# A hand-written beat table for the middle of a transformer block on one core: two alternating tables, and the split of keys or queries on GpSimd

## The chip, the core and the metric

The kernel runs on one core of one Trainium2 chip. The metric is device time in microseconds of one execution. Of the kernel before, three runs are known: 737.49, 738.01 and 738.19 us (median 738.01). A separate execution was profiled: 737.81 us, of which 736.0 us lie between its first and its last instruction.

Engines are named as the profile names them: PE (TensorE, the matmuls), PEld (its weight loads), DVE (VectorE), ACT (ScalarE), POOL (GpSimd), SP (SyncE, which here only issues DMAs).

## The reference: what is computed

One block of a diffusion transformer on x of 16 batches x 256 tokens x 256 features, in float32. The modulation vectors come from `cond`, 16 heads have 16 features each:

```python
x_norm = modulate(_ln(x), shift_a, scale_a)
q, k, v = jnp.split(x_norm @ W_qkv + b_qkv, 3, axis=-1)              # then 16 heads of 16
attn_w = softmax(einsum('bhqd,bhkd->bhqk', q, k) * scale)
x = x + gate_a[:, None] * (einsum('bhqk,bhkd->bhqd', attn_w, v) @ W_proj + b_proj)
q_c = _ln(x) @ W_qc + b_qc                                            # cross attention, 256 context rows
k_c, v_c = jnp.split(_ln(context) @ W_kvc + b_kvc, 2, axis=-1)
x = x + (softmax(q_c k_c * scale) v_c) @ W_cproj + b_cproj
h = gelu(modulate(_ln(x), shift_m, scale_m) @ W_mlp1 + b_mlp1) @ W_mlp2 + b_mlp2
x = x + gate_m[:, None] * h
```

## The kernel before

**Units.** An attention of one batch is a unit: 16 self attentions (names with `s`, `k`, `q`) and 16 cross attentions (names with `c`, `kc`, `qc`). They are done in the order of `seq` (line 785): five self attentions first, then self and cross attention in turn. From unit 5 to unit 25 an odd unit is a self attention and an even unit a cross attention. The MLP of all batches follows behind the units.

**High and low parts.** Matmuls run on float32r. To keep float32 accuracy an operand is cut in two: a high part that is rounded, and a low part, the rest (`xTh`/`xTl`, `h_k`/`l_k`, `h_q`/`l_q`). For a transposed activation ACT copies the PSUM tile to SBUF (`y`), POOL casts it to the high part and subtracts to get the low part (`cut`, line 380). For keys and queries ACT writes the high part (`high`, line 503: two ACTIVATE, bias added) and DVE the low part (`low`, line 508: two SCALAR_TENSOR_TENSOR that read PSUM and the high part). SP then sends rows of both by DMA into `big`, a stack in which 16 features of a head stand as three parts in 63 or 64 partitions (`send`, line 521).

**A unit's own work.** `s_tile` (line 691) multiplies queries by keys into two PSUM banks, `s` bank 0 and bank 1, and DVE takes the row maximum of each bank (`mx`, TENSOR_REDUCE). The maxima are transposed (`psm`), ACT negates them (`m`), and a DMA puts them as a 64th row into `big`. `t_part` (line 734) multiplies again, transposed and with the maximum subtracted, into `st`; ACT takes the exponent of the two halves of `st` in one instruction (`exp`, line 745, `pt`). `av_part` (line 768) multiplies by the values (`o`), ACT copies out (`oT`), PE transposes (`psA`), DVE divides by the row sums (`norm`, line 629), PE transposes again (`psT_a..`), and the projection follows (`ps_P`).

**Two lanes on PE.** Nearly all matmuls between have 64 rows, so that two run at once, one in each half of the array. `beside` (line 475) merges two lists of pieces, x for the upper half and y for the lower one, by the length issued so far; a matmul counts 1, a half transpose 0.53. PE takes them in this one order: a matmul that waits holds up both lanes.

**The beats.** A unit n is eight beats, and `PLAN` (line 1106) says what each holds: words before the lanes, the words of lane x, those of lane y, and words behind. Each beat has one `s` tile pair (of unit n+1) and one `t` pair (of unit n). Q12 is twelve matmuls of a lane of a projection (Q, K, V, P), T, U, A0, A1 and a are groups of half transposes, m0 and m1 those of the maxima; o0 (behind beat 4) and o1 (behind beat 0) are blocks of 16 matmuls with all four quarters of the array at work. The other words issue work of ACT, DVE, POOL or SP at that place: E the exponent of the beat, kh/kl/kH/kL and qh/ql/qH/qL the high and low parts of keys and queries (of unit n+2) and their DMAs, Te/Tc, Ue/Uc and ae/ac copies and cuts, n0/n1 the norms, c1/c2, e5/e6, s1/s6/s7 the three steps of layer norms, add and gate residual work of POOL, Vk the copy of V. Every engine takes its instructions in the order of the program (`InOrder`, line 40): a word's place decides what stands ahead of it on its engine.

The words that a sentence can't say:

```python
("c1", "s t Q12", "t P2 s P10", "L1 ld kL E"),          # beat 1 of PLAN, for odd and even units alike
("", "s t T pe A1 V3", "s t Q4 T A1 Q1", "hadd E L2 Te Tc c2"),
```

Of the kernel before, what the change touches and what calls it, by code (L numbers as in the profile page):

```python
# [16 lines left out]
P = 128  # L17
# [4 lines left out]
def pixart_block(  # L22
# [460 lines left out]
    def to_stack(W, src, bias, dst, which, name):  # L483
# [50 lines left out]
        o.low_pool = low_pool  # L534
        o.high, o.low = high, low
        o.send_high = lambda: [send(f, part) for part in range(2) for f in range(KC)]
# [63 lines left out]
    def build_post(u):  # L600
# [51 lines left out]
        def end():  # L652
            t1 = work.tile([P, NT, H], F32, tag="t1", name=f"t1_{name}")
            o.t1 = t1
            ACT.copy(t1.rearrange("p t h -> p (t h)"), o.ps)

        def add():
            t1 = o.t1
            if u.kind == "s":
# [96 lines left out]
    def exps():  # L756

        for f in later:
            f()
        later.clear()  # L760
# [133 lines left out]
    def to_hidden(b, c, src, park):  # L894
# [11 lines left out]

        o.high = o.keep = keep
        o.low = o.send_high = o.send_low = lambda: None
        return o
# [97 lines left out]
    for n, v in (("0", u0), ("1", u1), ("2", u2)):  # L1007
        word["T" + n + "t"], word["T" + n + "h"], word["T" + n + "l"] = v.T[0].parts
        word["T" + n + "p"] = v.T[0].low_pool
        for c in "KQ":  # L1010
# [4 lines left out]
            for f in range(KC):  # L1015
                for q, k in enumerate("xyl"):
                    word[f"{c}{n}{k}{f}"] = lambda o=o, q=q, f=f: o.send(f, q)
                    word[f"{c}{n}{k}{f}p"] = lambda o=o, q=q, f=f: o.send(f, q, POOL)
            word[c + n + "s"] = lambda o=o: [o.send(f, q) for f in range(KC) for q in range(3)]
    for n in range(2):  # L1020
# [71 lines left out]
    def visit(n, k, home=sp):  # L1092
# [6 lines left out]
        if n >= 0:  # L1099
            bank = sp if n == nu - 1 and k % 2 else st  # L1100
            t = [t_part(units[n], k, par, bank) for par in range(2)]
            later.append(lambda: exp(units[n], k, bank))
        return s, t

    none = (), ()
    PLAN = [
# [8 lines left out]
    ]  # L1115
    lanes = {}

    def beat(n, k):
# [21 lines left out]
        def attention(v, hf):  # L1140
# [6 lines left out]
        do = {  # L1147
            "E": exps, "o1": lambda: attention(prev, 1), "o0": lambda: attention(cur, 0),
            "kh": on(q2, lambda: q2.K.high()), "kl": on(q2, lambda: q2.K.low()),
# [7 lines left out]
            "ae": on(p1, lambda: p1.aT.evac()), "ac": on(p1, lambda: p1.aT.cut()),  # L1157
            "n1": on(p1, lambda: p1.norm(1)), "n0": lambda: cur.post.norm(0),
            "pe": on(p2, lambda: p2.end()), "hadd": on(p2 and (p2.n == nu - 3), lambda: (p2.add(), p2.store())),
            "add": on(p3, lambda: p3.add()), "gate": on(p1, lambda: p1.gate()),  # L1160
# [3 lines left out]
            "c1": on(lc or ls and ls.kind == "m", lambda: lc.ln[0].steps[0]() if lc else mlp_bias(ls.b)),  # L1164
            "c2": on(lc, lambda: [f() for f in lc.ln[0].steps[1:]]),
            "s1": on(ls, lambda: ls.ln[0].steps[0]()),
            "s6": on(ls, lambda: ls.ln[0].steps[1]()),
            "s7": on(ls, lambda: ls.ln[0].steps[2]()),
            "e5": on(early, lambda: early.ln[1].steps[0]()),
            "e6": on(early, lambda: [f() for f in early.ln[1].steps[1:]]),  # L1170
            "L1": on(late, lambda: lx.ln[1].steps[0]()), "L2": on(late, lambda: lx.ln[1].steps[1]()),
# [31 lines left out]

        before, x, y, then = PLAN[k]
        for w in before.split():
# [137 lines left out]
```

## Time and profile before

| | |
|---|---|
| three runs | 737.49, 738.01, 738.19 us |
| profiled execution | 737.81 us; span 736.0 us |
| PE busy | 727.4 us (99%), granted clock 0.999 |
| DVE, ACT, POOL busy | 567.6 (77%), 562.6 (76%), 521.6 us (71%) |
| DVE row maxima `mx<-s` | 504 instructions, 684 ns each |
| ACT exponents `pt<-st` | 252 instructions, 1027 ns each |

The span begins with some 45 us of set-up, the units fill the stretch to about 545 us, and the MLP the rest. The two `o` blocks of a unit are easily found in the chain of waits, so that they serve as milestones: those of unit 16 start at 303.7 and 311.8 us, of unit 17 at 319.7 and 328.0, of unit 18 at 335.9. A pair of units takes 32.25 us.

PE's busy share counts an instruction from its start to a modelled end, with two lanes overlapping, so 99% does not say that both lanes are filled: what a lane loses shows in the distance between the starts of its matmuls.

### The profile page before, as it was taken

How to read it: one execution, taken by the hardware profiler on the slowest of the kernel's cores; microseconds unless marked ns; L12 is line 12 of the kernel's file. 1: busy time of each engine (PE TensorE's matmuls, PEld its weight loads, DVE VectorE, ACT ScalarE, POOL GpSimd, SP SyncE). 2: the span in 40 equal slices, each digit the busy share in tenths (PEclk: the TensorE clock that was granted, in tenths of full speed). 3: DMA queues.
4: the chain of work that ended last, by engine and by line, in shares of the span. 5: the costliest groups of instructions: out<-in, count | busy, mean ns of one | idle time of the engine just before them, and what ended most of it. 6: DMA issues, size and time to landing. Idle time of an engine off the chain costs nothing.

```text
span 736.0 us, 25389 instructions
## 1 busy us (share of the span) xinstructions
PE 727.4 (99%) x10092; PEld 641.9 (87%) x10092; DVE 567.6 (77%) x1164; ACT 562.6 (76%) x976; POOL 521.6 (71%) x639
## 2 busy tenths in 40 slices
PE   8999999999999999999999999999999999999997
PEld 8778888888888888888888888888889999999997
DVE  5888888989888888888888989888746765565542
ACT  4277898888888888888888888888887766666663
POOL 6757576858567575856757687778568898898872
PEclk9999999999999999999999999999999999999999
DMA  6855445543545454354545555454321644443420
GB/s 207 204 148 146 134 129 137 141 124 97 155 112 157 131 143 136 103 153 112 159 129 138 139 143 164 121 164 121 118 74 30 166 134 110 121 129 92 118 81 33
DMA packets 108906, 94.81 MB, mean 129 GB/s; under 512 B 36914, under 2 KB 92756, under 8 KB 108788
## 3 DMA queue, kind: packets, MB, share of 16 engines
q1 hardware_dynamic: 108308, 92.27, 45.3%
q8 instruction: 80, 1.31, 0.8%
q0 software_dynamic: 192, 0.52, 0.3%
q10 hardware_dynamic: 288, 0.39, 0.2%
q14 instruction: 38, 0.31, 0.1%
HBM read 30.38 MB, written 11.86 MB: 57 GB/s over the span
## 4 chain that ended last, share of the span: by engine, by line
PE 94%; DVE 2%; issue 1%; ACT 1%; DMA 1%; POOL 1%; SPq 0%; POOLq 0%; ACTq 0%; DVEq 0%
PE s L51 17%; PE st L51 16%; PE o L51 16%; PE ph L51 11%; PE ps_qc L51 4%; PE ps_q L51 4%; PE ps_kc L51 3%; PE ps_P_s L51 3%; PE ps_k L51 3%; PE ps_v_c L51 3%; PE ps_v_s L51 3%; PE ps_P_c L51 2%; PE ps_h L51 1%; PE psT_q L51 1%; PE psA_s L51 1%
## 5 line engine op out<-in xcount | busy, mean ns | idle before, releaser
L51 DVE TENSOR_REDUCE mx<-s 128x2 f32<-128x512 f32 x504 | 324.6, 684 | 63.7 <-PE s L51 57.1
L51 ACT ACTIVATE pt<-st 128x1024 f32<-128x1024 f32 x252 | 258.9, 1027 | 17.7 <-PE st L51 11.8
L51 PE MATMUL s<-big 63*128 63x256 f32 (+1 forms) x1024 | 184.4, 298 | 0.6 <-DVE mx L51 0.4
L51 PEld LDWEIGHTS s<-big 63*128 63x128 f32 (+1 forms) x1024 | 133.6, 186 | 19.9 <-DVE l_kc L51 6.6
L51 PE MATMUL st<-big 64*128 64x256 f32 (+1 forms) x1024 | 134.2, 298 | 0.3 <-ACT pt L51 0.2
L51 PE MATMUL o<-pt,v 128*32 128x256 f32 x2048 | 123.8, 382 | 0.1
L51 PEld LDWEIGHTS st<-big 64*128 64x128 f32 (+1 forms) x1024 | 96.0, 185 | 16.2 <-issue 12.9
L51 POOL TENSOR_TENSOR hl<-hf,hh 128x512 fp32r<-128x512 f32 x64 | 85.1, 1335 | 29.1 <-ACT hh L51 29.0
L51 PEld LDWEIGHTS o<-pt,v 128*32 128x32 f32 x2048 | 60.2, 109 | 41.4 <-PE psm L51 0.2
L51 ACT ACTIVATE hh<-ph,bT 128x256 fp32r<-128x256 f32 x114 | 47.8, 473 | 23.3 <-PE st L51 10.0
L51 ACT ACTIVATE hf<-ph,bT 128x256 f32<-128x256 f32 x114 | 47.6, 469 | 21.2 <-PE ph L51 21.2
L51 ACT COPY oT<-o 128x512 f32<-128x512 f32 x63 | 36.9, 586 | 33.9 <-PE o L51 33.9
L51 PE MATMUL s<-big,hh 128*128 128x256 f32 x256 | 46.8, 282 | 0.0
L51 PE MATMUL st<-big,hh 128*128 128x256 f32 x256 | 46.5, 281 | 0.0
L51 PE MATMUL ph<-wqch,wself 128*128 128x256 f32 x224 | 44.4, 282 | 0.0
L51 PE MATMUL ph<-wkch,wself 128*128 128x256 f32 x224 | 44.3, 281 | 0.0
L51 PE MATMUL ps_k<-xTh_s,wself 64*128 64x256 f32 (+1 forms) x232 | 43.9, 294 | 0.0
L51 DVE TENSOR_SCALAR xn_m<-x,mv_m,rs_m 128x256 f32<-128x256 f32 x28 | 28.8, 1067 | 19.0 <-POOL rs_m L51 19.0
L51 POOL CAST xTh_ac<-y_ac 128x512 fp32r<-128x512 f32 x15 | 9.2, 612 | 46.6 <-ACT y_ac L51 46.6
L51 POOL CAST xTh_c<-y_c 128x512 fp32r<-128x512 f32 x16 | 9.8, 612 | 45.5 <-ACT y_c L51 45.5
L51 PE MATMUL ps_q<-xTh_s,wself 64*128 64x256 f32 (+1 forms) x240 | 39.8, 283 | 0.4 <-DVE l_q L51 0.4
L51 PE MATMUL ps_v_s<-wself,xTh_s 64*128 64x256 f32 x224 | 39.2, 294 | 0.0
(249 smaller groups left out, 2528.5 us busy)
## 6 DMA issues: line engine op xcount, KB each, us to landing
big<-h_kc SPq DMA_DIRECT2D x64, 128.0 KB
big<-h_qc SPq DMA_DIRECT2D x64, 128.0 KB
big<-h_k SPq DMA_DIRECT2D x62, 128.0 KB
big<-h_q SPq DMA_DIRECT2D x62, 128.0 KB
big<-l_k SPq DMA_DIRECT2D x32, 128.0 KB
big<-l_q SPq DMA_DIRECT2D x32, 128.0 KB
g<-gd SPq DMA_DIRECT2D x16, 256.0 KB
c<-in_ctx_dram SPq DMA_DIRECT2D x16, 256.0 KB
```

The source lines that it names most:

```text
L51: i = f(*a, **k)
```

## The change

Units 6 to 21 (8 even, 8 odd) are done by two new tables, `PLANS[0]` for even n and `PLANS[1]` for odd n; the other units keep the old table, which is now `PLANS[2]`. All words of the old table stay in each of the new ones, but their places differ, many now stand inside a lane, and four steps are changed:

- **Keys of even units (`kr`, `kc`) and queries of odd units (`qr`, `qc`).** With `rows` ACT writes the rows with bias as float32 to SBUF (two ACTIVATE as before), with `cut` POOL casts them to the high part and subtracts for the low part. The two DVE instructions of `low` are gone there. Queries of even units and keys of odd units are made as before.
- **F** issues the exponent as two instructions, one for each half of `st`, in place of one (twice a unit).
- The layer norms' middle step is parted: statistics (DVE) apart from the power (POOL): c2/c3/c4, s6/s7/s8, e6/e7/e8.
- Lane lengths of some beats differ (Q, V and K matmuls moved over a beat's edge).

`gated_end`, the words pd, add2, store2 and the sends by ACT are defined and not used by the tables.

```diff
@@ to_stack
+        def rows():
+            o.hi = work.tile([P, KC, N], F32R, tag="qkh", name=f"h_{name}", bufs=3)
+            o.lo = work.tile([P, KC, N], F32R, tag="qkl", name=f"l_{name}", bufs=3)
+            for f in range(KC):
+                ACT.activation(o.lo[:, f].bitcast(F32), o.ps[:, f * N:(f + 1) * N], AF.Identity, bias=bias[f])
+
+        def cut():
+            POOL.tensor_copy(o.hi, o.lo.bitcast(F32))
+            POOL.tensor_tensor(o.lo, o.lo.bitcast(F32), o.hi, ALU.subtract)
@@ exp
-    def exp(u, pair, st):
+    def exp(u, pair, st, apart=False):
         u.pt[pair] = work.tile([P, 2, NT, N], F32, tag="pt", name=f"pt_{u.n}_{pair}", bufs=5)
-        if isinstance(st, list):
+        if apart or isinstance(st, list):
             for r in range(2):
-                ACT.activation(u.pt[pair][:, r].rearrange("p c n -> p (c n)"), st[r], AF.Exp, scale=SCALE)
+                ACT.activation(u.pt[pair][:, r].rearrange("p c n -> p (c n)"), side(st, r), AF.Exp, scale=SCALE)
             return
@@ the tables
-    PLAN = [
+    FROM, TO = 6, 22
+    PLANS = [[("", "s t kr m1 E", "m1 add t s", "m1s"),
+              ("kc o1", "s t Q12", "t s P12 E c1", "gate"),
...
+              ("", "t e5 ql s a m0 K6", "t s V4 a V2 m0 F", "ae"),
...
+              ("", "s Te V1 t V1 hadd Tc F V7", "Q2 t s Q5 qr", ""),
+              ("qc", "s t qH", "s t", "E c4 L3 o0"),
+              ("", "t store s a E K2 m0 K2", "n1 t s qL V4 a V1 m0", "ae ac s1 e5 m0s"),
+              ("", "s lc K1 t K3 A0 E K4 U", "V3 t begin V2 s U s6 V2 e8 A0", ""),
...
@@ beat
-        before, x, y, then = PLAN[k]
+        before, x, y, then = PLANS[n % 2 if FROM <= n < TO else 2][k]
```

What the tables move is seen in the order of the engines' instructions. First DVE in unit 16 (even), from behind beat 4 to beat 7; `l_qc` is the low part of queries, `st_q`/`mv_q` the statistics of a layer norm, `mx<-s_110` and `mx<-s_111` the maxima of the two banks. Before:

```order
L51 SCALAR_TENSOR_TENSOR l_qc_6649<-ps_qc_6488,bT,h_qc_6611 128x256 x2
L51 TENSOR_REDUCE mx_83<-s_110 128x2
L51 TENSOR_REDUCE mx_83<-s_111 128x2
L51 BN_STATS st_q_6703<-xg_4229 128x6 x2
L51 TENSOR_REDUCE mx_83<-s_110 128x2
L51 TENSOR_REDUCE mx_83<-s_111 128x2
L51 BN_AGGR mv_q_6740<-st_q_6703 128x2 x2
```

And in the changed kernel:

```order
L51 BN_STATS st_q_6674<-xg_4277 128x6 x2
L51 SCALAR_TENSOR_TENSOR l_qc_6677<-ps_qc_6499,bT,h_qc_6633 128x256 x2
L51 TENSOR_REDUCE mx_83<-s_110 128x2
L51 TENSOR_REDUCE mx_83<-s_111 128x2
L51 BN_AGGR mv_q_6725<-st_q_6674 128x2 x2
L51 TENSOR_REDUCE mx_83<-s_110 128x2
L51 TENSOR_REDUCE mx_83<-s_111 128x2
```

The statistics went ahead of the maxima of beat 5, to where PE is in its `o` block, and the aggregation ahead of those of beat 6.

Second, POOL in the first beats of unit 16; `t_s`, `xg` are the residual work of a self attention (words add and gate), `xTh_s`/`xTl_s` the parts that the K matmuls of unit 19 read in beat 5, `rs_c` a layer norm's power. Before:

```order
L51 TENSOR_TENSOR t_s_6157<-t_s_6157,g_5614 128x512
L51 TENSOR_TENSOR xg_5723<-xg_5723,t_s_6157 128x512
L51 TENSOR_TENSOR xg_6470<-x_4638,g_6361 128x512
L51 CAST xTh_s_6565<-y_s_6562 128x512
L51 TENSOR_TENSOR xTl_s_6566<-y_s_6562,xTh_s_6565 128x512
L51 TENSOR_SCALAR rs_c_6572<-mv_c_6569 128x2
L51 TENSOR_TENSOR rs_c_6572<-rs_c_6572,mhalf 128x2
```

And in the changed kernel:

```order
L51 TENSOR_TENSOR t_s_6156<-t_s_6156,g_5595 128x512
L51 TENSOR_TENSOR xg_5779<-xg_5779,t_s_6156 128x512
L51 CAST h_kc_6457<-l_kc_6458 128x512
L51 TENSOR_TENSOR l_kc_6458<-l_kc_6458,h_kc_6457 128x512
L51 TENSOR_TENSOR xg_6530<-x_4651,g_6346 128x512
L51 TENSOR_SCALAR rs_c_6582<-mv_c_6579 128x2
L51 TENSOR_TENSOR rs_c_6582<-rs_c_6582,mhalf 128x2
L51 CAST xTh_s_6599<-y_s_6576 128x512
L51 TENSOR_TENSOR xTl_s_6600<-y_s_6576,xTh_s_6599 128x512
```

The split of the keys `h_kc`/`l_kc` is new in this queue, and it and the power now stand ahead of the cast `xTh_s`.

Third, PE in unit 17 (odd), at the edge from beat 2 to beat 3; `psA` are half transposes of lane y, `ps_q` matmuls of lane y, `ps_v` of lane x. Before:

```order
L51 MATMUL psA_c_6906<-ident,oT_3_6837 128x64 x3
L51 MATMUL ps_q_6853<-xTh_s_6565,wself 128x256
L51 MATMUL s_110<-big_75 128x256
L51 MATMUL ps_q_6853<-xTh_s_6565,wself 128x256
L51 MATMUL s_110<-big_75 128x256
L51 MATMUL st<-big_77 128x256 x4
```

And in the changed kernel:

```order
L51 MATMUL psA_c_6927<-ident,oT_3_6859 128x64 x4
L51 MATMUL s_110<-big_75 128x256
L51 MATMUL ps_q_6872<-xTh_s_6599,wself 128x256
L51 MATMUL s_110<-big_75 128x256
L51 MATMUL ps_q_6872<-xTh_s_6599,wself 128x256
L51 MATMUL ps_v_s_6934<-wself,xTh_s_6599 128x256
L51 MATMUL st<-big_77 128x256 x4
```

A matmul of `ps_v` now stands ahead of `st`, and one of `ps_q` went from ahead of `psA` to behind `s`.

More of the change, by code (lines that the diff above doesn't have):

```diff
@@ L534, in to_stack @@
         o.low_pool = low_pool
-        o.high, o.low = high, low
+        o.high, o.low, o.rows, o.cut = high, low, rows, cut
         o.send_high = lambda: [send(f, part) for part in range(2) for f in range(KC)]
@@ L653, in end, with gated @@
             t1 = work.tile([P, NT, H], F32, tag="t1", name=f"t1_{name}")
-            o.t1 = t1
+            o.t1, o.gated = t1, False
             ACT.copy(t1.rearrange("p t h -> p (t h)"), o.ps)
+        def gated():
+            o.t1 = o.out = work.tile([P, NT, H], F32, tag="t1", name=f"t1_{name}")
+            o.gated = True
+            ps = o.ps.rearrange("p (t h) -> p t h", t=NT)
+            if u.kind == "s":
+                DVE.tensor_tensor(o.t1, ps, bc_t(G[b][:, 0]), ALU.mult)
+            else:
+                DVE.tensor_tensor(o.t1, ps, X1[b], ALU.add)
+        o.gated_end = gated
         def add():
             t1 = o.t1
+            if o.gated:
+                if u.kind == "s":
+                    X1[b] = o.xg
+                    POOL.tensor_tensor(X1[b], o.xg, t1, ALU.add)
+                return
             if u.kind == "s":
@@ L754, in pixart_block, with exps @@
     later = []
-    def exps():
+    def exps(apart=False):
         for f in later:
-            f()
+            f(apart)
         later.clear()
@@ L905, in keep @@
             M[b].kept.append(c)
-        o.high = o.keep = keep
-        o.low = o.send_high = o.send_low = lambda: None
+        o.high = o.keep = o.rows = keep
+        o.low = o.cut = o.send_high = o.send_low = lambda: None
         return o
@@ L1018, in pixart_block @@
                     word[f"{c}{n}{k}{f}p"] = lambda o=o, q=q, f=f: o.send(f, q, POOL)
+                    word[f"{c}{n}{k}{f}a"] = lambda o=o, q=q, f=f: o.send(f, q, ACT)
             word[c + n + "s"] = lambda o=o: [o.send(f, q) for f in range(KC) for q in range(3)]
@@ L1101, in visit @@
             t = [t_part(units[n], k, par, bank) for par in range(2)]
-            later.append(lambda: exp(units[n], k, bank))
+            later.append(lambda apart: exp(units[n], k, bank, apart))
         return s, t
     none = (), ()
-    PLAN = [
[8 rows of a table removed]
-    ]
+    FROM, TO = 6, 22
+    PLANS = [[("", "s t kr m1 E", "m1 add t s", "m1s"),
[23 rows of a table added]
     lanes = {}
@@ L1158, in beat @@
             "n1": on(p1, lambda: p1.norm(1)), "n0": lambda: cur.post.norm(0),
+            "pd": on(p2, lambda: p2.gated_end()), "kr": on(q2, lambda: q2.K.rows()), "kc": on(q2, lambda: q2.K.cut()),
+            "qr": on(q2 and hasattr(q2, "Q"), lambda: q2.Q.rows()), "qc": on(q2 and hasattr(q2, "Q"), lambda: q2.Q.cut()),
+            "add2": on(p2, lambda: p2.add()), "store2": on(p2, lambda: p2.store()),
             "pe": on(p2, lambda: p2.end()), "hadd": on(p2 and (p2.n == nu - 3), lambda: (p2.add(), p2.store())),
```

12 lines of the change are left out of this document (7 added, 5 removed), and 25 rows, old and new, of tables (PLAN, PLANS).

## The prediction

> **What bounds the kernel now.** I read the page first, then the windows between the `o` blocks, then the timelines of single engines. The page says that PE is busy all the time, so the question is how well its two lanes are filled. The windows of one pair (units 16 and 17; columns: window, its length, then busy time of PE, PEld, DVE, ACT, POOL) run from the end of an `o` block to the next; the blocks themselves, of which one row stands here, take 1.86 or 1.87 us each:
>
> ```profile
> 305.55:311.85 6.30, 6.29 (x105) 5.90 (x101) 5.40 (x14) 5.24 (x9) 4.76 (x9) 1.00 0.37 102
> 311.85:313.71 1.86, 1.86 (x35) 0.93 (x33) 1.83 (x4) 1.65 (x3) 1.75 (x2) 1.00 0.00 0
> 313.71:319.74 6.03, 6.03 (x100) 5.78 (x96) 4.57 (x9) 5.18 (x8) 1.62 (x2) 1.00 0.54 156
> ...
> 321.61:328.03 6.42, 6.41 (x113) 6.15 (x109) 5.40 (x14) 5.76 (x10) 3.82 (x6) 1.00 0.65 171
> ...
> 329.89:335.93 6.04, 6.04 (x101) 5.80 (x97) 5.27 (x13) 5.43 (x9) 5.69 (x6) 1.00 0.51 134
> sum 32.25, PE 32.24 PEld 27.37 DVE 28.06 ACT 27.21 POOL 21.32; mean PE 4.03 PEld 3.42 DVE 3.51 ACT 3.40 POOL 2.66
> ```
>
> I call the four stretches P (beats 5 to 7 of the even unit and beat 0 of the odd one, 6.30 us), Q (beats 1 to 4 of the odd unit, 6.03), R (beats 5 to 7 of the odd unit and beat 0 of the even one, 6.42) and S (beats 1 to 4 of the even unit, 6.04). DVE, ACT and POOL sum to 28.1, 27.2 and 21.3 us of 32.25: none is full, but DVE and ACT are close enough to make PE wait in places.
>
> A lane that waits for nothing issues at a steady pace. Twelve `ps_q` matmuls of one lane:
>
> ```profile
> 314.29 0.28 PE L51 MATMUL ps_q<-xTh_s,wself 64*128 64x256 f32 x1
> ...
> 315.58 0.28 PE L51 MATMUL ps_q<-xTl_s,wself 64*128 64x256 f32 x1
> ```
>
> Eleven steps in 1.29 us: 0.117 us a slot. By the old table the longer lane of P counts 12.6 + 12.1 + 16 + 4.5 = 45.2 slots, 5.29 us; R has the four half transposes U more, 47.3 slots, 5.54 us; Q and S count 16 + 13.2 + 13 + 4 = 46.2 slots, 5.41 us. What is left is idle: P 1.01, Q 0.62, R 0.88, S 0.63 us, together 3.1 us a pair. Eight pairs of units use the new tables, so about 25 us is the ceiling of any gain.
>
> **Part by part.** *The low parts that leave DVE* are worth nothing by themselves. In the old order they run while PE is in an `o` block:
>
> ```profile
> 304.69 0.87 DVE L51 SCALAR_TENSOR_TENSOR l_qc<-ps_qc,bT,h_qc 128x256 fp32r<-128x256 f32 x2
> 306.32 1.29 DVE L51 TENSOR_REDUCE mx<-s 128x2 f32<-128x512 f32 x2 [0.76 <-PE s L51]
> 307.53 0.74 DVE L51 BATCH_NORM_STATS2 st_q<-xg 128x6 f32<-128x256 f32 x2
> 308.19 1.27 DVE L51 TENSOR_REDUCE mx<-s 128x2 f32<-128x512 f32 x2
> ```
>
> Behind `l_qc` DVE idles 0.76 us until the first maximum of beat 5. Of each pair 2 x 0.87 us leaves DVE, and what counts is only what takes the free place. Were the cover gone, each would cost its 0.87 us.
>
> *Stretch P.* The statistics (0.74 us) move into that hole and the maxima of beat 6, which started at 308.19, can start about 0.44 us earlier. But what holds the lanes in beat 7 is ACT:
>
> ```profile
> 308.00 1.02 ACT L51 ACTIVATE pt<-st 128x1024 f32<-128x1024 f32 x1
> 308.93 0.57 ACT L51 COPY v<-ps_v_c 128x512 f32<-128x512 f32 x1
> 309.65 0.35 PE L51 MATMUL ps_P_s<-wself,xTh_as 64*128 64x256 f32 x1
> ```
>
> The projection takes over the PSUM buffer of V, whose copy ends at 308.93 + 0.57 = 309.50; `ps_P_s` follows at 309.65, and twelve slots of it end the beat. The new table keeps this copy behind the exponents of beats 5 and 6, and the one of beat 5 is now two instructions. Their price isn't in this place of the trace; the last unit has the split form:
>
> ```profile
> L51 ACT ACTIVATE pt<-st 128x1024 f32<-128x1024 f32 x252 | 258.9, 1027 | 17.7 <-PE st L51 11.8 <-PE s L51 0.2
> L51 ACT ACTIVATE pt<-s 128x512 f32<-128x512 f32 x8 | 4.4, 605 | 0.2 <-PE s L51 0.2
> ```
>
> The eight fill 4.4 us, so a pair of halves takes 1.1 us (1.21 if nothing overlapped) where one instruction takes 1.03: 0.07 to 0.18 us later, and below nothing only if lane x gains more from its half being free sooner. I take the lower end, since consecutive ACT rows overlap here: +0.07 us for P. The maxima gain nothing there.
>
> *Stretch Q.* At the edge of beats 2 and 3:
>
> ```profile
> 316.47 1.03 ACT L51 ACTIVATE pt<-st 128x1024 f32<-128x1024 f32 x1
> 316.68 0.38 PE L51 MATMUL ps_v_s<-wself,xTh_s 64*128 64x256 f32 x1
> 316.90 0.28 PE L51 MATMUL ps_v_s<-wself,xTh_s 64*128 64x256 f32 x1
> 317.26 0.28 PE L51 MATMUL s<-big 63*128 63x256 f32 x1
> 317.55 0.51 PE L51 MATMUL st<-big 64*128 64x256 f32 x4
> ```
>
> `st` waits for the exponent (316.47 + 1.03 = 317.50), and lane x stands from 317.26 + 0.12 to its `st`; a V matmul now fills a slot of that: -0.1. The first V waits, and the step behind a wait is 0.22 us in place of 0.12; one more Q matmul now stands ahead of it: -0.1. F in beat 3 gains nothing, since beat 4 still waits for its bank's maximum. Q: -0.2 us, with 0 and -0.4 as ends.
>
> *Stretch R.* Beat 5 loses and beat 6 gains lane work, and U in lane y now stands far from U in lane x. Before, the second half of U waited for the first:
>
> ```profile
> 324.81 0.22 PE L51 MATMUL psA_s<-ident,oT 64*128 64x64 f32 x1
> 325.04 0.27 PE L51 MATMUL psT_q<-ident,xn_q 64*128 64x64 f32 x1
> 325.87 0.28 PE L51 MATMUL ps_P_c<-wcph,xTh_ac 64*128 64x256 f32 x1
> 324.97 0.58 ACT L51 COPY v<-ps_v_s 128x512 f32<-128x512 f32 x1
> ```
>
> A step of 0.23 us stands where a half transpose takes half a slot, 0.06 (-0.17); the new table's lanes count 11.6 + 16.2 + 16 + 4.5 = 48.3 slots, one more (+0.12). Of the 0.88 us that idle here I credit another 0.15 to the longer beat 6, in which PE has work while DVE is at the statistics; that is a choice between 0 and what V's copy allows: the projection, now at 325.87, can't come before 324.97 + 0.58 = 325.55, so the whole gain ends at 0.3. R: -0.2 us.
>
> *Stretch S.* The same wait of the first V (-0.1) and beat 4's wait for the maxima of beat 3, which one `s` slot earlier shortens (-0.1); lane x of beat 3 has V10, which makes 47.2 slots (+0.12). The statistics `c1` went from ahead of beat 1's maxima to behind them, where DVE idles:
>
> ```profile
> 332.31 1.29 DVE L51 TENSOR_REDUCE mx<-s 128x2 f32<-128x512 f32 x2 [0.57 <-PE s L51]
> ```
>
> 0.74 us (as `st_q` above) in a hole of 0.57 plus the time that `c1` gives back ahead of beat 1: nothing. S: -0.1 us.
>
> *POOL* gets two splits a pair, ahead of `xTh_s`, which beat 5's K waits for:
>
> ```profile
> 302.17 0.61 POOL L51 CAST xTh_s<-y_s 128x512 fp32r<-128x512 f32 x1 [0.25 <-PE s L51]
> 302.86 1.30 POOL L51 TENSOR_TENSOR xTl_s<-y_s,xTh_s 128x512 fp32r<-128x512 f32 x1
> 304.25 0.22 POOL L51 TENSOR_SCALAR rs_c<-mv_c 128x2 f32<-128x2 f32 x1
> 304.55 0.72 POOL L51 TENSOR_TENSOR rs_c<-rs_c,mhalf 128x2 f32<-128x2 f32 x1
> 305.25 0.24 POOL L51 TENSOR_SCALAR less_c<-mv_c 128x2 f32<-128x2 f32 x1
> 306.42 0.35 PE L51 MATMUL ps_k<-xTh_s,wself 64*128 64x256 f32 x1
> ```
>
> Start to start a split costs 304.25 - 302.17 = 2.08 and a power 305.25 - 304.25 = 1.00 us: the cast would end at 302.78 + 3.08 = 305.86, with K at 306.42: hidden by 0.56 us. The Trainium skill, page "Perfetto Trace Analysis", section "GPSIMD Engine Instruction", says that a GpSimd span in a profile is unreliable and that start-to-start spacing is to be used; by the spans alone the delay would be 0.61 + 1.30 + 0.22 + 0.72 = 2.85 us and the margin 0.79. The rows above agree with it: a cast of 0.61 us is followed 0.69 us later.
>
> The DMAs of split keys and queries leave later, behind POOL's cast and subtraction; they are due in beat 0 of the next unit. SP is in order, so the maxima rows `m` queue behind the queries' low parts:
>
> ```profile
> 306.04 1.18 SPq L51 DMA_DIRECT2D big<-l_qc  x2
> 307.94 5.14 SPq L51 DMA_DIRECT2D big<-m  x2
> ```
>
> SP is free for 0.7 us between the two, and the `st` that reads this `m` stands in beat 0, half a microsecond ahead of the `o` block at 311.85, over 3 us later. I take nothing; if `m` were late by a whole pair of issues, 1.18 us, PE would still have 2 us.
>
> Sum: +0.07 - 0.2 - 0.2 - 0.1 = -0.43 us a pair, times eight -3.4 us. From the profiled execution's 737.8 that is 734.4; that execution lies 0.2 us under the median of the three runs and within them, so I leave it. A difference of about 0.2% (1.5 us) is what a measurement of this kernel can tell from no change.
>
> **Rivals.** *Slots paid, waits kept (slower).* The waits I strike out are kept because a matmul behind V's copy or the exponent comes no sooner, whatever stands ahead of it; the two extra slots (0.23 us) and the split exponent (0.07 us) are paid: +0.30 x 8 = +2.4, 740.2 us. It decides if fewer than 0.30 of my 0.73 us of struck-out waits go. For it speaks that P's gain is already eaten by ACT; against it the step of 0.23 us at U, which is PE's own wait.
>
> *GpSimd late (slower).* POOL starts a chain in R and, with the two splits, has no pause up to K in the next P:
>
> ```profile
> 323.88 0.61 POOL L51 CAST xTh_ac<-y_ac 128x512 fp32r<-128x512 f32 x1 [3.85 <-ACT y_ac L51]
> 316.14 1.29 DVE L51 TENSOR_REDUCE mx<-s 128x2 f32<-128x512 f32 x2 [0.60 <-PE s L51]
> ```
>
> K of the next pair is at 306.42 + 32.25 = 338.67, so the chain has 14 us. If its instructions run a tenth slower, 1.4 us, K waits 1.4 - 0.56 = 0.84 us a pair: (0.84 - 0.43) x 8 = +3.3, 741.1 us; it decides from 7% on. The Trainium skill, "Perfetto Trace Analysis", section "Optimizing Scalar/DVE Operations", says that moving work between DVE and GpSimd may not help since they share an SBUF port. The trace doesn't show it for the maxima: two take 1.29 us at 316.14, in a stretch where POOL works 1.62 us, and 1.29 us at 332.31, where it works 5.69 of 6.04 us.
>
> *Half of all idle lanes filled (faster).* The tables reach more places than I followed: 1.55 x 8 = 12.4, 725.4 us. For it: DVE has room in all stretches; against: ACT's share doesn't fall.
>
> *Waits only change places.* What ends earlier at one beat waits at the next `o` block: 737.8 us.
>
> **Chances.** Forecast 0.50, half of all idle 0.13, no difference 0.14, slots paid 0.13, GpSimd late 0.10. Faster 0.63, same 0.14, slower 0.23. The forecast's own range is its terms' ends: Q 0 to -0.4, R +0.1 to -0.3, S +0.1 to -0.3, P +0.18 to 0, or about +0.1 to -0.9 a pair, 731 to 738. The whole range reaches to 727 and 740.5, which leaves out part of the large gain and of late GpSimd.
>
> **What would show it.** The same windows: P as long as before or longer, with `ps_P_s` still right behind V's copy; R 0.2 us shorter, without the step of 0.23 us at U; `l_k` of even and `l_q` of odd units on POOL. PE idle behind POOL's `xTh_s` in beat 5 would show GpSimd late; Q, R and S as long as before would make the slots' rival right; a shorter P would make me wrong on ACT.

## The result and the profile after

The changed kernel takes 747.59 us (median of 6 runs, 743.90 to 749.38); the kernel before took 738.10 us on the same chip (median of 6 runs, 737.49 to 739.01). The ratio is 1.0114, with a 95% interval from 1.0090 to 1.0138: slower by over 1%, where 734.4 us was forecast, and outside the range. The runs of the changed kernel also scatter over 5.5 us, those of before over 1.5.

The page of the changed kernel: span, instructions, and the engines' busy time.

```profile
span 745.6 us, 25418 instructions
PE 732.0 (98%) x10092; PEld 644.5 (86%) x10092; DVE 558.5 (75%) x1132; ACT 562.2 (75%) x1008; POOL 552.0 (74%) x671
```

This says little: PE is as full as before. A better ruler is the unit, from its first `o` block to the first `o` block of the next unit. The table gives, for units 6 to 21, the length before and after, and for the changed kernel when the queries' low parts (`l_qc` in even, `l_q` in odd units) and the maxima rows `m` are issued on SP, in us behind the start of the unit's first `o` block. The last column is the start, counted in the same way, and the length of a DMA packet of 16 KB in the queue that the trace calls "instruction", if one lies 1 to 8.5 us behind that start; it matters below. (A second queue of that name moves 37 packets of 8 KB, which are left out.)

| unit | before | after | low parts | m | packet of 16 KB |
|---|---|---|---|---|---|
| 6 | 16.04 | 16.91 | 4.2 | 5.5 | 5.5 (1.31) |
| 8 | 16.04 | 16.65 | 4.2 | 6.2 | 4.2 (0.91) |
| 10 | 16.05 | 16.27 | 4.1 | 5.3 | 2.0 (0.96) |
| 12 | 16.06 | 16.73 | 5.0 | 6.2 | none |
| 14 | 16.06 | 20.31 | 5.4 | 6.7 | 7.2 (1.56) |
| 16 | 16.06 | 16.02 | 2.9 | 4.2 | 4.6 (1.04) |
| 18 | 16.05 | 16.21 | 3.4 | 5.7 | 4.0 (1.26) |
| 20 | 16.07 | 16.96 | 5.2 | 6.5 | none |
| 7 | 16.23 | 16.18 | 3.5 | 4.8 | 4.6 (1.17) |
| 9 | 16.16 | 17.08 | 4.2 | 6.7 | 4.7 (1.24) |
| 11 | 16.38 | 16.15 | 4.2 | 5.5 | none |
| 13 | 16.18 | 16.19 | 4.3 | 5.6 | 7.4 (1.36) |
| 15 | 16.23 | 17.78 | 4.2 | 5.4 | 5.7 (1.76) |
| 17 | 16.18 | 17.07 | 4.2 | 6.6 | 4.9 (1.19) |
| 19 | 16.18 | 16.17 | 4.3 | 5.5 | 1.6 (0.88) |
| 21 | 16.19 | 16.22 | 4.2 | 5.5 | none |

Units 6 to 21 together take 268.9 us where they took 258.2: all of the loss is here. It is not spread evenly. Units 16, 7, 11, 13, 19 and 21 are about as long as before, 10 and 18 some 0.2 us longer, the others 0.6 to 4.3 us. Before, the low parts left 2.3 to 3.9 us behind the `o` block and `m` 4.2 to 5.2.

Unit 14, the worst, shows how the delay comes about. POOL in its beats 0 to 3 (start, busy time, operation): the residual's two operations (`t_s`, `xg`) stand ahead of the split of the keys.

```profile
268.55 1.30 POOL L51 TENSOR_TENSOR t_s<-t_s,g 128x512 f32<-128x512 f32 x1
269.93 1.30 POOL L51 TENSOR_TENSOR xg<-xg,t_s 128x512 f32<-128x512 f32 x1
271.15 0.63 POOL L51 CAST h_kc<-l_kc 128x512 fp32r<-128x512 f32 x1
271.86 1.28 POOL L51 TENSOR_TENSOR l_kc<-l_kc,h_kc 128x512 fp32r<-128x512 f32 x1
```

SP's queue in the same unit, whose first `o` block starts at 274.06:

```profile
271.81 3.65 SPq L51 DMA_DIRECT2D big<-h_kc  x4
275.56 1.19 SPq L51 DMA_DIRECT2D big<-l_kc  x2
276.85 2.47 SPq L51 DMA_DIRECT2D big<-h_qc  x4
279.42 1.20 SPq L51 DMA_DIRECT2D big<-l_qc  x2
280.71 6.19 SPq L51 DMA_DIRECT2D big<-m  x2
```

The keys' first transfer leaves 2.3 us ahead of the `o` block, where it left 6.5 to 6.7 ahead before. With it begin twelve transfers of 128 KB, with no gap over 0.1 us between these rows, so `l_qc` leaves at 5.4 and `m` at 6.7 us behind the `o` block. The four issues of `h_kc` take 3.65 us here and the four of `h_qc` 2.47: a packet of 16 KB, 1.42 us long, begins at 272.37, and the issue under way ends only behind it (more on this below). In the prediction's rows of before they left at 306.04 - 303.68 = 2.4 and 307.94 - 303.68 = 4.3. Over the whole stretch SP's waits were (released by whom, us in total, times, longest):

```profile
SPq L51 <- ACT m L51: 52.0, 16, 5.0
SPq L51 <- POOL h_kc L51: 20.5, 7, 3.4
SPq L51 <- POOL h_q L51: 16.5, 8, 3.4
```

In the chain of waits of unit 14, DVE's last work is done at 281.95 and PE does nothing until 284.10, when the first `s` of beat 0 (the products of the keys and queries just sent) can start:

```profile
281.52 0.43 DVE A_c L51
281.95 2.15 issue
284.10 0.28 PE s L51
```

The chain says "issue", which means that the profile names no one for this wait; that it is a transfer is read from what follows.

The view of the DMAs from 281.2 to 284.2 (40 slices; share of 16 engines in tenths, then GB/s) shows what PE waits for:

```profile
DMA  4957889663210000000001000010010000000000
GB/s 150 369 123 177 191 246 259 219 205 96 68 48 21 0 0 0 0 0 0 0 0 14 0 14 0 14 14 14 0 14 14 14 27 0 0 0 0 0 0 0
q8 instruction: 1, 0.02, 3.2%
```

At 282.2 all is moved but a few packets, which come singly from 282.8 to 283.7, at 14 GB/s in a slice of 0.075 us: 1 KB each. The one packet of the instruction queue takes 3.2% of 16 engines over 3.0 us, 1.54 us, as long as the packet in the trace that starts at 281.30 and ends at 282.86. The ten packets of 1 KB begin at 282.85, each about as the one ahead of it ends, and the last is through at 283.72. That fits one DMA engine of sixteen being held for 1.5 us, with the rest of `l_qc` queued behind it; the trace does not name the engine. PE needs the whole transfer.

### The profile page after: what moved, and what is told of

Read it like the earlier page. It is cut to its first block, busy times and chain, and to the rows that moved or that the text cites. A ratio compares the mean times of both kernels' runs of the same rounds, so it can differ in the third digit from the quotient of the medians.

```text
span 745.6 us, 25418 instructions
## 1 busy us (share of the span) xinstructions
PE 732.0 (98%) x10092; PEld 644.5 (86%) x10092; DVE 558.5 (75%) x1132; ACT 562.2 (75%) x1008; POOL 552.0 (74%) x671
## 3 DMA queue, kind: packets, MB, share of 16 engines
q8 instruction: 80, 1.31, 0.8%
## 4 chain that ended last, share of the span: by engine, by line
PE 91%; DVE 4%; issue 2%; DMA 1%; ACT 1%; POOL 1%; SPq 0%; POOLq 0%; DVEq 0%; ACTq 0%
PE s L51 18%; PE st L51 16%; PE o L51 15%; PE ph L51 11%; PE ps_q L51 4%; PE ps_qc L51 4%; PE ps_kc L51 3%; PE ps_v_c L51 3%; PE ps_v_s L51 3%; PE ps_k L51 2%; PE ps_P_s L51 2%; DVE mx L51 2%; PE ps_P_c L51 2%; PE ps_h L51 1%; PE psA_s L51 1%
## 5 line engine op out<-in xcount | busy, mean ns | idle before, releaser
L51 ACT ACTIVATE pt<-st 128x1024 f32<-128x1024 f32 (+1 forms) x284 | 261.1, 931 | 25.3 <-PE st L51 13.0
L51 PE MATMUL s<-big 63*128 63x256 f32 (+1 forms) x1024 | 191.1, 300 | 5.7 <-issue 3.8
L51 PEld LDWEIGHTS s<-big 63*128 63x128 f32 (+1 forms) x1024 | 136.2, 186 | 26.1 <-issue 8.4
L51 PE MATMUL st<-big 64*128 64x256 f32 (+1 forms) x1024 | 139.3, 300 | 1.3 <-DMA big<-m 0.9
L51 PEld LDWEIGHTS st<-big 64*128 64x128 f32 (+1 forms) x1024 | 99.2, 186 | 17.8 <-issue 14.6
L51 PE MATMUL ps_k<-xTh_s,wself 64*128 64x256 f32 (+1 forms) x232 | 46.6, 300 | 0.0
L51 DVE TENSOR_SCALAR xn_m<-x,mv_m,rs_m 128x256 f32<-128x256 f32 x28 | 31.0, 1147 | 19.1 <-POOL rs_m L51 19.1
L51 PE MATMUL ps_v_s<-wself,xTh_s 64*128 64x256 f32 x224 | 40.9, 294 | 0.0
L51 PEld LDWEIGHTS st<-big,hh 128*128 128x128 f32 x256 | 39.0, 188 | 0.0
```

What stands on the lines that cost most here:

```text
L51: i = f(*a, **k)
```

## The experiments

**Which part.** The theory: keys that wait for POOL hold up everything behind them in SP's order, and beat 0 waits for it. Rivals: the odd units' queries; the order of the tables itself. Four kernels, compared with the changed kernel's 747.6.

*keys_back:* in the table of even units

```
-("", "s t kr m1 E", ...), ("kc o1", ...
+("", "s t kh m1 E", ...), ("kl o1", ...
```

> The keys of even units made as in the kernel before (high part by ScalarE, low part by VectorE); everything else as changed. The changed kernel is 9.5 us over the kernel before (747.6 against 738.1), and in its trace the lost time stands ahead of the second o block of even units, where s or st wait for a transfer: SyncE sends the queries and the maxima rows m behind the keys, and the keys wait for GpSimd's cast, which stands behind the residual's two operations. Theory 'keys late in SyncE's order': 738 to 741 us, units 14 and 15 without the step of 2.6 us, SyncE's wait for GpSimd's h_kc (20.5 us between 142 and 402) gone. Rival 'queries of odd units are late': 746 to 749. Rival 'the tables' order itself, or the exponents made apart': 745 to 749.

Measured: 742.02 us (741.03 to 743.82), 1.0056 of before, interval 1.0042 to 1.0071. Of the 9.5 us lost, 5.6 come back. All even units but one are 16.01 to 16.03 us, 0.03 shorter than before; unit 10 has 16.29. The late ones left are odd: 9, 15, 17 and 19 with 16.75, 17.14, 17.18 and 16.40 us. That is 1 us over the range expected: the theory holds for the even units and isn't all.

*queries_back:* in the table of odd units

```
-("", ..., "Q2 t s Q5 qr", ""), ("qc", "s t qH", ...
+("", ..., "Q2 t s Q5 qh", ""), ("ql", "s t qH", ...
```

> The queries of odd units made as in the kernel before; the keys of even units still split on GpSimd. Theory 'keys late in SyncE's order': 745 to 748 us, a part of it at most, since the queries of odd units have nothing behind them but m. Rival 'queries of odd units are late': 738 to 741. Rival 'the tables' order itself': 745 to 749.

Measured: 751.50 us (750.50 to 753.23), ratio 1.0178, interval 1.0148 to 1.0208: 3.9 us slower than the changed kernel, which no theory had expected. Every odd unit has 16.96 to 17.31 us, and the even ones are still late (16.40 to 19.63).

*both_back:* both edits.

> Keys and queries both made as in the kernel before, so that the two tables' order stands alone. Theory 'keys late in SyncE's order': 734 to 739 us; below 738 if the struck-out waits of the prediction are worth something, 738 if they are not. Rival 'the tables' order itself, or the exponents made apart': 744 to 749, as the changed kernel.

Measured: 743.75 us (742.90 to 744.97), ratio 1.0072, interval 1.0045 to 1.0099. That is far over the range of the theory and just under the rival's. Even units have 16.00 to 16.03, odd units 16.91 to 17.04, all eight alike. In the new order the queries' low part on VectorE costs each odd unit some 0.77 us (16.95 on average, against 16.18 in the run early, below, which has it on POOL; units 7, 11, 13 and 21 of keys_back, which differ from these by the queries alone and are not late, have 16.18 to 16.25). DVE at the change from beat 4 to beat 5 of unit 17:

```profile
322.85 0.88 DVE L51 SCALAR_TENSOR_TENSOR l_q<-ps_q,bqkv,h_q 128x256 fp32r<-128x256 f32 x2 [0.99 <-ACT h_q L51]
323.64 1.28 DVE L51 TENSOR_REDUCE mx<-s 128x2 f32<-128x512 f32 x2
324.83 0.25 DVE L51 RECIPROCAL rc_c<-psA_c 128x16 f32<-128x16 f32 x1
325.11 0.42 DVE L51 TENSOR_TENSOR A_c<-psA_c,rc_c 128x256 f32<-128x256 f32 x1
```

and PE behind it:

```profile
325.68 0.24 PE L51 MATMUL psT_ac<-ident,A_c 64*128 64x64 f32 x1 [0.21 <-DVE A_c L51]
```

In this table `l_q` stands ahead of beat 4's maxima, and it must wait for ScalarE first; the maxima, the normalisation `A_c` and the transposes behind it all come later. So with the low part at this place of the table (that of `qc`) the split on POOL pays for itself in odd units, and only there; a place behind the `o` block, as in the old table, was not tried in the new one.

*add_behind:* the changed kernel with one word moved in the table of even units:

```
-("", "s t kr m1 E", "m1 add t s", "m1s"), ("kc o1", ...
+("", "s t kr m1 E", "m1 t s", "m1s"), ("kc add o1", ...
```

> The changed kernel with the residual's operations (word add, 2.6 us on GpSimd) behind the split of the keys in even units instead of ahead of it. The split ends up to 2.6 us earlier, and every send behind it on SyncE with it. Theory 'keys late in SyncE's order': 738 to 742 us. Rivals 'queries of odd units' and 'the tables' order itself': 745 to 749, no change.

Measured: 740.87 us (739.53 to 741.88), ratio 1.0034, interval 1.0021 to 1.0047. The keys leave 4.9 to 5.7 us ahead of the `o` block instead of 2.2 to 3.9, `l_qc` 2.4 to 3.0 and `m` 4.2 to 4.3 behind it, and seven of the eight even units have 16.00 to 16.03 us. SP's wait for the keys is down from 20.5 to 3.1 us:

```profile
SPq L51 <- POOL h_q L51: 12.7, 8, 2.3
...
SPq L51 <- POOL h_kc L51: 3.1, 6, 0.7
```

The late units left are odd (most of all 15 with 17.60 and 19 with 16.87), but for unit 10 with 16.28.

**The odd units, and the exponents.**

*early:* add_behind, and in the table of odd units

```
-("qc", "s t qH", "s t", "E c4 L3 o0"),
-("", "t store s a E K2 m0 K2", "n1 t s qL V4 a V1 m0", "ae ac s1 e5 m0s"),
+("qc", "s t qH", "s t", "E c4 L3 o0 qL"),
+("", "t s a E K2 m0 K2", "n1 t s V4 a V1 m0", "ae ac s1 e5 m0s store"),
```

> The changed kernel with the residual's operations behind the keys' split (as in the run add_behind, 740.9 us), and in odd units the queries' low parts sent right behind beat 4 and the store of the residual moved from ahead of them in SyncE's order to behind m. In add_behind the even units had 16.01 us each and the odd units 16.18 to 17.60; l_q left 4.1 us and m 5.4 us after the first o block of an odd unit, against 2.4 and 4.25 in the kernel before. Theory 'transfers with too little slack': l_q and m leave some 0.7 to 0.8 us earlier, so most irregular stalls of odd units go: 738 to 739.5 us. Rival 'the lost time of odd units is something else than the queries' transfers': 740.5 to 741.5, as add_behind.

Measured: 737.18 us (736.30 to 739.02, 11 runs), ratio 0.9993, interval 0.9984 to 1.0002. `l_q` leaves at 3.5 us (4.0 in unit 19), and no unit is late: even ones 16.01 to 16.14, odd ones 16.15 to 16.25. Changes of order alone give back all that was lost; below the kernel before it is by nothing that can be told apart.

*early_one_exp:* `E` for each `F` in early.

> The kernel of the run early, with one exponent instruction over a pair's 128x1024 instead of two over 128x512 at the four places a pair where the tables have them apart. By the prediction's price, 0.07 us of ScalarE each and only one of the four in the sum, it is within 0.6 us of early either way if the exponents made apart are no cause; rival 'the exponents made apart cost': 1 to 3 us faster than early.

Measured: 737.53 us (736.65 to 738.03), ratio 0.9983, interval 0.9965 to 1.0001. Within 0.4 us of early: the split exponents are no cause.

*late_low:* the kernel before, with `qL` moved from the end of beat 4 to the end of beat 5 in units 6 to 21.

> The kernel before with nothing changed but that units 6 to 21 send the queries' low parts one beat later, behind beat 5 and just ahead of m, so that they leave about 4.3 us after the first o block instead of 2.4, and m 5.5 instead of 4.3; no table of beats is new, and GpSimd gets nothing. Theory 'transfers with too little slack': irregular stalls of 0.3 to 1.5 us ahead of the second o block in those units in which a 16 KB fetch of instructions (about one in 8 us, 0.9 to 1.8 us long in the trace) falls on the transfer: 739 to 744 us. Rival 'the tables' order or GpSimd's work is the cause': 737.5 to 738.6, no change.

Measured: 738.20 us (737.27 to 741.38), ratio 1.0006, interval 0.9996 to 1.0016. A miss of the experiment: the low parts left at 2.4 us as before. A send that moves past no other send changes nothing, since SP waits for data and not for a place in the table. It tells neither way.

*pad:* the changed kernel with 64 matmuls of 128x8 ahead of everything.

> The changed kernel with 64 small matmuls (128 instructions with their weight loads, which is half of one 16 KB fetch) ahead of everything, so that every later fetch falls at another place of the program. In the changed kernel's trace unit 14 lasts 20.3 us and unit 15 17.8, with a fetch of 1.56 us just ahead of the first stall and one of 1.76 us ahead of the second. Theory 'a fetch of instructions holds up one DMA engine': other units are the long ones, 14 is no longer the longest by far. Rival 'the order alone decides which units are late': 14 and 15 are again the longest. The time itself is some 3 to 8 us more for the added matmuls.

Measured: 774.85 us in a single execution; unit 14 has 19.70 us and 15 has 17.32. By its words the rival wins, but the trace counts 128 more matmuls and 128 more weight loads, 256 instructions, and between two packets of 16 KB lie about 250 such records of PE on average: the shift was a whole packet, and the packets stand at the same places of the units (unit 14: 7.6, unit 15: 5.7). It has to be made with half of that.

**Packets and lateness.**

*pad_half:* the changed kernel with 32 such matmuls.

> The changed kernel with 32 small matmuls ahead of everything. The 64 of the run pad were 256 instructions, since each of them is two matmuls and two weight loads in the trace, so the fetches of 16 KB fell on the same places of the units again; 32 are 128 instructions, half a fetch, 4 us. In the runs so far the odd units whose l_q left 4.1 to 4.3 us after the first o block were late where a fetch began 4.6 to 5.8 us after it (units 9, 15 and 17) and not where none did (units 11, 13 and 21). Theory 'a fetch that holds up one DMA engine decides among late units': units 9, 15 and 17 now within 0.1 us of 16.2, and late ones among 11, 19 and 21, where the fetch should come instead. Rival 'the order alone decides which units are late': 9, 15 and 17 again 0.4 to 1.6 us long.

Measured: 763.85 us in a single execution, 19 us of it ahead of the units (unit 6 starts at 161.3 instead of 141.9 us; from 8 to 35 us of the set-up the granted clock is 0.50 here and 1.00 in the changed kernel). In the odd units:

| unit | after | its packet | pad_half | its packet |
|---|---|---|---|---|
| 9 | 17.08 | 4.7 (1.24) | 16.32 | none |
| 11 | 16.15 | none | 17.35 | 4.8 (1.61) |
| 13 | 16.19 | 7.4 (1.36) | 16.52 | 4.0 (1.13) |
| 15 | 17.78 | 5.7 (1.76) | 16.71 | 1.2 (1.04) |
| 17 | 17.07 | 4.9 (1.19) | 16.26 | none |
| 19 | 16.17 | 1.6 (0.88) | 17.42 | 6.0 (1.46) |
| 21 | 16.22 | none | 16.84 | 4.9 (1.01) |

9 and 17 are well, 11, 19 and 21 are late: as the theory had it. Unit 15 has no packet on its last transfers and is still 0.5 us late; its `l_q` leaves at 4.7 instead of 4.2. Over the run PE's waits name the transfers:

```profile
PE s L51 <- DMA big<-l_q: 1.0, 1, 1.0
PE st L51 <- DMA big<-m: 1.0, 4, 0.3
```

The traces also show that a packet acts on SP itself. In units 6 to 21 of the changed kernel twelve issues of rows for `big` take over 0.8 us, where nearly all others take 0.53 to 0.61 (none over 0.79). Each of the twelve overlaps a packet of 16 KB and ends 0.38 or 0.39 us behind the packet's end; in the kernel before the same holds for fourteen (0.28 to 0.41 us). Unit 17 of the changed kernel, whose packet lasts from 333.11 to 334.30:

```profile
332.35 2.34 SPq L51 DMA_DIRECT2D big<-l_q  x2
334.77 0.55 SPq L51 DMA_DIRECT2D big<-m  x1
```

Unit 15 of pad_half, whose packet lasts from 312.06 to 313.10:

```profile
311.78 3.01 SPq L51 DMA_DIRECT2D big<-h_q  x4
```

In unit 17 of pad_half, with no packet in the way, the two issues of `l_q` take 1.18 us and the four of `h_q` 2.48. So a packet delays a unit in two ways: it can hold the arrival of a transfer that has left (units 14 and 15 of the changed kernel), or an issue, and with it all that stands behind it on SP (`m` at 6.6 and 6.7 in units 17 and 9). That is also why unit 15 is late here: its packet, at 1.2 us, held an issue of `h_q`, and in the chain of waits `m`, issued at 316.81, lets `st` start at 318.84. Units 12 and 20 of the changed kernel, "none" in the first table, have packets at 0.5 and 0.8 us that held an issue of `l_kc` for 1.28 and 1.16 us; so their low parts left at 5.0 and 5.2 and not at 4.2.

*add_behind_pad:* add_behind with the 32 matmuls.

> The kernel of the run add_behind with the same 32 small matmuls ahead of everything. Theory 'a fetch that holds up one DMA engine decides among late units': units 9, 15 and 17, which had 16.61, 17.60 and 16.54 us, are within 0.1 us of 16.2, late ones are among 11, 19 and 21; even units 16.0 us. Rival 'the order alone decides': 9, 15 and 17 again late.

Measured: 760.10 us in a single execution. Units 9 and 17 have 16.33 and 16.17 us, 11, 13, 19 and 21 have 16.78, 17.14, 17.53 and 16.65, unit 15 has 16.59 with `l_q` at 4.6. Even units 16.00 to 16.11 but for unit 10 (16.29). The same picture; unit 15 again has its packet at 1.2 us.

*late_q1:* the kernel before, with `ql` between the maxima of beat 5 and `qL` ahead of `m0s`.

> The kernel before with one edit in units 6 to 21: VectorE makes the queries' low parts behind the maxima of beat 5 instead of ahead of them, and they are sent behind beat 5, just ahead of m. In the run late_low only the place of the sends was moved, and SyncE issued them as early as before (2.4 us after the first o block), since nothing stood between; here the data itself comes later, so that l_q should leave at about 4.5 us and m at about 5.8. Theory 'transfers with too little slack': stalls of 0.3 to 1.5 us ahead of the second o block in several of the sixteen units, 740 to 748 us. Rival 'lateness of the low parts and of m is not enough, the new order or GpSimd's work is needed': 737.5 to 739.

Measured: 781.99 us (781.26 to 783.11), ratio 1.0586, interval 1.0554 to 1.0617. It is no test of the transfers, though they left at 4.4 and 6.4 us: the low part is also what frees the PSUM buffer of the queries' projection, and the next keys' projection takes that buffer over.

```profile
PE ps_k L51 <- DVE l_qc L51: 13.3, 7, 1.9
PE ps_kc L51 <- DVE l_q L51: 13.2, 7, 1.9
```

*dose3, dose5:* the kernel before, and three or five more transfers of 128 KB in units 6 to 21, behind the queries' high part (word `qX` behind `qH` in beat 4), into memory that nothing reads:

```
+for _ in range(3):          # five in dose5
+    SP.dma_start(void[void_at[0]], o.hi[:, 0].bitcast(F32))
+    void_at[0] += 1
```

> The kernel before, and in units 6 to 21 three more transfers of 128 KB each on SyncE between the queries' high and low parts; they write the high part to memory that nothing reads, so no other engine's work or order is touched. At 0.6 us for an issue, l_q should leave about 4.2 us after the first o block instead of 2.4, and m about 5.4 instead of 4.3, which is where the odd units of the changed kernel have them. Theory 'transfers with too little slack, and a fetch that holds up one DMA engine': stalls of 0.3 to 1.6 us ahead of the second o block in those units in which a 16 KB fetch begins 4 to 6 us after the first (units 6, 7, 9, 15, 16, 17 and 18 in the trace of before), none in the others: 739.5 to 745 us. Rival 'the new order or GpSimd's work is needed for the loss': 737.5 to 738.6.

Measured: 746.14 us (745.01 to 747.41), ratio 1.0112, interval 1.0096 to 1.0128: the loss of the changed kernel, in the order of before and with no split on POOL. Low parts leave at 4.0 to 4.9, `m` at 5.3 to 6.9. Units 12 and 14, with the low parts at 4.1 and 4.0 and no packet near, have 16.05 and 16.06 us; the seven units named have 16.33 to 17.37. "None in the others" was too much: the packet now also falls on unit 8 (4.9 us, 16.76), and low parts that leave at 4.4 to 4.9 us cost 0.1 to 0.5 us without one (unit 19, 4.9: 16.70). The added transfers also keep the DMA engines busy; units 12 and 14 show that this alone costs nothing, but in the other units it isn't told apart from the later issue. The chain of unit 17:

```profile
330.15 3.73 DMA big<-l_q
333.88 0.35 PE s L51
```

> The same with five more transfers: l_q should leave about 5.4 us after the first o block and m about 6.6, as in unit 14 of the changed kernel. Theory 'transfers with too little slack': nearly every one of the sixteen units is late, by 0.4 to 1 us without a fetch (as units 12 and 20 of the changed kernel) and by up to 4 us with one: 746 to 765 us. Rival 'the new order or GpSimd's work is needed for the loss': 737.5 to 739.

Measured: 770.31 us (767.03 to 773.48), ratio 1.0453, interval 1.0424 to 1.0483: every unit is late, by 0.8 to 3.7 us, and the time lies above the range expected; the waits name the same three transfers.

```profile
PE st L51 <- DMA big<-m: 5.2, 13, 1.2
PE s L51 <- DMA big<-l_q: 3.8, 4, 1.2
PE s L51 <- DMA big<-l_qc: 3.5, 4, 1.3
```

## Why the prediction was wrong

**The step that failed** is the last of the part-by-part section: "The DMAs of split keys and queries leave later, behind POOL's cast and subtraction ... SP is free for 0.7 us between the two ... I take nothing". That term was put at nothing; in the traces the sixteen units are 10.7 us longer, 1.3 us a pair. Its bound on the delay of `m`, 1.18 us, was nearly right: where no packet holds an issue (units 6, 11, 13, 15 and 21), `m` leaves at 5.4 to 5.6 us, against 4.2 to 4.3 in most units of before, and units 11, 13 and 21 lose nothing. Three things were missing. The low parts leave 1.8 us later (4.2 against 2.4), in even units since the keys are sent behind a cast that stands behind the residual's 2.6 us on POOL; the first `s` of beat 0 reads them and can stand still ahead of the `st` that the step looked at. Packets of instructions hold issues on SP, so that `m` leaves up to 2.4 us later than before (6.7 in unit 14). And the step took the time of the issue for that of the arrival, where arrival has a tail: some 1.5 us in unit 14, where a packet fell on the transfer. The runs give the slack: low parts that leave by 3.5 us cost 0.3 us at most, with a packet or without (unit 7 of add_behind, 16.40; unit 6 of early_one_exp, 16.32); at 4.0 to 4.3 they cost 0.15 us at most without one (unit 10 aside) and mostly 0.3 to 1.6 us with one that begins 4 to 6 us behind the `o` block; from 4.4 on they often cost something without one. The odd units of queries_back and both_back are left out here, which are long for another reason.

**The stretches.** With the transfers in time (early) the new order can be seen, with the splits on POOL in it. Its windows, from the end of an `o` block to the next, answer to P, Q, R and S of units 16 and 17:

```profile
306.06:312.32 6.26, 6.26 (x105) 5.95 (x101) 5.50 (x13) 5.23 (x10) 5.75 (x10) 1.00 0.41 113
314.18:320.21 6.03, 6.03 (x101) 5.73 (x97) 4.17 (x7) 5.18 (x9) 2.15 (x3) 1.00 0.51 144
322.07:328.51 6.44, 6.44 (x112) 6.22 (x108) 5.44 (x13) 5.69 (x10) 4.12 (x8) 1.00 0.75 221
330.38:336.37 5.99, 5.99 (x100) 5.77 (x96) 5.35 (x13) 5.37 (x10) 5.83 (x6) 1.00 0.47 125
```

Before they were 6.30, 6.03, 6.42 and 6.04 us. P: -0.04 where +0.07 was forecast, Q: 0.00 for -0.2, R: +0.02 for -0.2, S: -0.05 for -0.1; together -0.07 a pair for -0.43. Some waits that were to go did go, the half transposes' in R among them, but others came: in Q `s` of beat 4 waits for the maxima of beat 3 (0.35 us on one lane, 0.23 before), as this row of DVE in early shows from the other side.

```profile
319.97 1.29 DVE L51 TENSOR_REDUCE mx<-s 128x2 f32<-128x512 f32 x2 [0.48 <-PE s L51]
```

DVE and PE wait for each other there in turn, which fits that an earlier V matmul moves nothing. In R the credit of 0.15 us for beat 6, called a choice, can't have been there in full; which waits took the gains of R and S was not followed up. The outcome is that of the rival *waits only change places* (737.2 measured, 737.8 forecast). The forecast's own range was also too narrow for its working: the ends of its four terms add up to -1.0 and +0.38 us a pair, 729.8 to 740.8 us, where it said 731 to 738.

**The low parts that leave DVE.** "Worth nothing by themselves" holds in even units (keys_back 16.02, add_behind 16.01). In odd ones it is wrong in the new order: 0.77 us. The working counted the cover of the old order, an `o` block with DVE idle behind it; the tables took that cover away, and the text had named its price, 0.87 us.

**POOL.** K's cast was hidden, as forecast: in unit 14 `xTh_s` starts at 275.45 and takes 0.61 us, and K's first matmul comes at 276.81, 0.75 us behind its end. The rival *GpSimd late* (741.1) had the right engine and sign, but the wrong reader: POOL was late not for K but for SP's queue.

**The split exponents**, +0.07 us in the sum, make no difference that can be measured (early against early_one_exp).

**What would show it.** The list named waits of PE for POOL, DVE and ACT, and none for a transfer, so the one that decided was not on it.

What stays open: why a packet holds an issue on SP; on which of the sixteen engines it lies, which is inferred from shares and stragglers and not seen; and unit 10, late by 0.25 us in three of these kernels. Its delay arises behind the second `o` block (in add_behind at 15.85 us, where `st` waits for an exponent that ScalarE began late), so it isn't the low parts.

## What to carry to other kernels

An engine off the critical path that makes what a DMA sends moves every later send of that DMA queue, so follow the queue to its end and compare, for each transfer, the time at which it leaves with the time at which its first reader stands. Count slack up to arrival, with a tail, and not up to the issue: here 1.1 us more at the issue cost 0.3 us at most, and 1.8 us cost up to 1.6. The length of an issue isn't fixed either. Where a step leaves an engine, price it in the new order: what hid it may have been moved by the same change.

## What was not expected of the hardware

Packets of the queue that the trace calls "instruction" hold up the transfers of the kernel's data. Those of 16 KB come about every 8 us and take 0.88 to 1.76 us in units 6 to 21 of the changed kernel; about 250 matmuls and weight loads lie between two of them, and 32 matmuls (128 records) put ahead of everything moved them by half their distance. The Trainium skill, "DMA: Bandwidth & Descriptors", section "Why a DMA increments its semaphore by 16 and not by 1", says that a transfer runs on up to 16 engines that finish independently and that only the full count means that all data has landed. The trace agrees: with all but a few packets of `l_qc` landed at 282.2 and the last at 283.72, `s` starts at 284.10.

A stall can also cost clock. PE stood for 2.4 us in unit 14 (281.66 to 284.10), and the windows around it (length, busy times of PE, PEld, DVE, ACT, POOL, then the granted clock) show what follows:

```profile
281.90:284.10 2.20, 0.00 (x0) 0.03 (x1) 0.04 (x1) 0.64 (x2) 2.10 (x5) 1.00 0.05 12
284.10:286.00 1.90, 1.90 (x26) 1.27 (x30) 1.35 (x3) 1.05 (x2) 0.51 (x1) 0.85 0.00 0
286.00:288.00 2.00, 2.00 (x22) 0.69 (x14) 0.72 (x2) 0.30 (x2) 0.00 (x0) 0.50 0.01 4
288.00:290.00 2.00, 2.00 (x31) 2.00 (x30) 1.21 (x2) 1.47 (x2) 0.00 (x0) 0.79 0.52 138
290.00:292.00 2.00, 2.00 (x45) 2.00 (x43) 1.40 (x3) 1.53 (x3) 0.00 (x0) 1.00 0.78 197
```

The clock falls after the stall, to half speed: 0.15 x 1.90 + 0.50 x 2.00 + 0.21 x 2.00 = 1.7 us of PE are lost, on top of the stall, and the unit's 4.25 us come mostly from the two. At half speed throughout, 1.7 us lost are 3.4 us long, and the trace's record of the clock has 0.50 from 285.41 to 288.83, 3.42 us. The Trainium skill, "TensorE: Matmul & The Clock Gate", section "What's actually happening", gives that length, about 3.4 us, for the window by which the clock is set, and asks for an idle window; the trace agrees with the length and the half speed, but here 2.4 us without a matmul were enough. Shorter stalls did it in other runs: in late_q1 PE stands sixteen times for 1.9 us, and the clock is at 0.50 for 3.42 us behind eight of them, in those units that take 19.35 to 19.65 us where the others take 18.16 to 18.30. The stall of unit 15, 1.37 us on one lane, cost no clock: the windows there stay at 1.00. The length of the stall alone doesn't decide.
